# RWKV recurrence on one core: keys repeated by TensorE into PSUM, values repeated by DMA

## The chip, the cores and the metric

The kernel runs on one core of one Trainium2 chip. The metric is the device time of one execution in microseconds (us); the time before is the median of three runs. The core has five engines that work side by side and wait for each other by semaphores: TensorE (PE) multiplies matrices and writes to PSUM, VectorE (DVE) and ScalarE (ACT) work elementwise on SBUF and PSUM, GpSimd (POOL) elementwise on SBUF, and SyncE (SP) issues DMAs, as ACT does for stores.

## What is computed

Four layers run one after the other on x of 16 x 100 x 512 (fp32): a cross-attention (layer 0), an RWKV block (1), a second cross-attention with its feed-forward (2), and another RWKV block (3). The change touches the RWKV blocks alone. Their core, per batch, for 32 heads of 16 channels:

```python
def step(s, rkvw):
    r_t, k_t, v_t, w_t = rkvw
    a = k_t[..., :, None] * v_t[..., None, :]
    out = jnp.einsum('bhi,bhij->bhj', r_t, u * a + s)
    s = a + w_t[..., :, None] * s
    return (s, out)
...
_, out = jax.lax.scan(step, s0, rkvw)
```

Each head has a state of 16 x 16 (key channel i, value channel j) that decays by w and gains k times v in each of 100 time steps; r reads it out. Before it stand a layer norm, a mix with the previous step and projections to r, k, v, w and the gate g; after it a group norm, the gate, the output projection, and a channel mix (feed-forward).

## The kernel before

`rwkv` takes 16 batches in 4 groups of G = 4, so T = 400 columns (batch, time) in each tile. The 512 channels are 4 chunks of 128; chunk C of all 16 (group, chunk) pairs is 8 units, so there are 128 units a layer. A unit is two planes of 128 partitions x 400 columns: each partition is one (key channel, value channel) pair of a head, and one scan instruction of DVE runs its recurrence over the columns. Time step 0 of each batch has a decay of 0, so that four batches stand in one scan.

A unit has these steps, with the lines of the kernel before:

- `spread(u)` (L1132): two matmuls with 32 rows each write v, repeated by a selection matrix `sel` over the partitions, to the PSUM tile `vb` (two tiles of two banks each, in turn), shifted by one time step. ACT then copies the initial state s0 (`s0r`) to the first column of each batch.
- `product(u)` (L1147): DVE multiplies `vb` in place by `kr`, the keys repeated over the partitions.
- `scan(u)` (L1156): DVE runs two scans, with the decays `wr` and the products in `vb`, into the SBUF tile `a`; POOL multiplies `a` by `rr`, the repeated receptances.
- `gather(p)` (L1166): for each pair of units, four matmuls add the products up over the key channels to the PSUM bank `acc`. After a chunk, `norm` (L1178) reads it.
- `bonus` (L1110) adds the term with u.

The repeated `kr`, `wr` and `rr` come from DRAM: the projections are stored there (`store`, L806, issued by ACT) and loaded by SP in `enter` (L1089, plain tiles `kc`, `vc`, `rc`) and `repeat` (L1099: three tensors, four DMAs each, for half a chunk of four units). `gates` (L1203) loads g.

The units share the engines with all the rest of the block. A loop over u (L1231) writes the order of every engine out by hand: instructions on PE, DVE, ACT and POOL stay in program order (`keep_in_program_order`), while SP's DMAs may be put in order by the framework. In each turn the loop emits the steps of the units, then takes "pieces" from a list (projections of the next group, output projection, channel mix) until a budget `due` in us is used up. Three PSUM banks (`slots`) serve the pieces; a bank that DVE reads is read one turn later (`slots.begin`). The tails of a turn's pieces are therefore read by DVE ahead of the next unit's scans.

```python
due = min(due, 0.0) + (2.5 if 0 <= u < 29 else 2.95 if u < UNITS - 32 else 3.9)
due -= 0.45 * (u % 2) + 0.7 * (at in (2, 7)) if unit else 0.0
```

Of the kernel before, what the change touches and what calls it, by code (L numbers as in the profile page):

```python
# [17 lines left out]
G = 4  # L18
# [17 lines left out]
def xattn_sequence(ctx: ExitStack, tc: tile.TileContext, d: dict, out: bass.AP):  # L36
# [42 lines left out]
    vector, scalar, gpsimd = InOrder(nc.vector), InOrder(nc.scalar), InOrder(nc.gpsimd)  # L79
# [556 lines left out]
    def rwkv(n, ws, next_weights, last):  # L636
# [6 lines left out]
        with ExitStack() as es:  # L643
# [6 lines left out]
            vbs = [psum.tile([128, 2, 512], F32, name=f"vb{i}") for i in range(2)]  # L650
            acc = psum.tile([128, 512], F32, name="acc")
            slots = Slots([psum.tile([128, 512], F32, name=f"mm{i}") for i in range(3)])
            vec = rwkv_vecs(one, n)
# [35 lines left out]
            fold = one.tile([128, 32], F32, name="fold")  # L689
            nc.vector.tensor_reduce(fold, ident.rearrange("p (r s) -> p s r", s=32), AX.X, ALU.add)  # L690
            sel = one.tile([128, 16, 32], F32, name="sel")
            for j in range(16):
                nc.vector.tensor_copy(
                    sel[:, j, :].rearrange("p (h i) -> p h i", i=16),
                    fold.rearrange("p (h j) -> p h j", j=16)[:, :, j : j + 1].to_broadcast([128, 2, 16]),
                )


            share = one.tile([128, 2], F32, name="share")
            nc.vector.tensor_reduce(share, heads8.rearrange("p (q h) -> p h q", h=2), AX.X, ALU.add)  # L700
# [3 lines left out]
            for jg in range(4):  # L704
                nc.vector.tensor_copy(
                    gat[:, jg, :].rearrange("p (h g q) -> p g q h", g=4, q=4)[:, jg],
                    heads8.rearrange("p (q h) -> p q h", h=2),
                )
                nc.vector.tensor_tensor(
                    gat[:, jg, :].rearrange("p (h j) -> p h j", j=16),  # L710
                    gat[:, jg, :].rearrange("p (h j) -> p h j", j=16),
                    share[:, :, None].to_broadcast([128, 2, 16]), ALU.add,
                )

            s0r = one.tile([128, 4, NC, 4, B], F32, name="s0r")
            for r in range(4):
                rs = slice(32 * r, 32 * r + 32)
                ps = slots.bank()
                for c in range(NC):
                    for jq in range(4):  # L720
                        mm(
                            out=ps[32 * jq : 32 * jq + 32, c * 64 : (c + 1) * 64], lhsT=ident[rs, rs],
                            rhs=s0[rs, c].rearrange("p b (g q) -> p q g b", q=4)[:, jq],
                            start=True, stop=True,
                        )
                scalar.copy(s0r[:, r].rearrange("p c g b -> p (c g b)"), ps[:, : NC * 64])

            steps = lambda t: t.rearrange("p (b t) -> p b t", t=L)
            stage = lambda name: two.tile([128, 512], F32, tag="stage", bufs=6, name=name)
# [6 lines left out]
            nws = {}  # L736

# [60 lines left out]

            def projections(g, base):
                nm = f"{n}_{g}"  # L800
                to = put[g] = {
                    t: dram.tile([NC, 4, 32, T], F32, tag=t, name=f"d{t}_{nm}")
                    for t in ("k", "v", "r", "w", "g")
                }

                def store(t, c, tile):  # L806
                    nc.scalar.dma_start(out=to[t][c].rearrange("r p t -> (r p) t"), in_=tile)
# [83 lines left out]
                def plain(f, w, t, co):  # L891
                    def read(ps):
                        out = stage(f"{t}_{nm}_{co}")
                        scalar.copy(out[:, :T], ps[:, :T])
                        store(t, co, out[:, :T])

# [74 lines left out]
            def channels(g, slot):  # L971
# [41 lines left out]
                def keys(co):  # L1013
                    def read(ps):
                        if co == 0:
                            st["kk"] = two.tile([128, NC, T], F32, tag="kk", bufs=1, name=f"kk_{nm}")
# [19 lines left out]
                def values(i):  # L1036
                    b = g * G + i

                    def read(ps):
                        def add():  # L1040
# [3 lines left out]
                            if last:  # L1044
                                nc.sync.dma_start(out=out[b], in_=xb[b])
# [41 lines left out]
            products = {}  # L1087

            def enter(C):  # L1089
# [4 lines left out]
                for k, bufs in (("v", 2), ("k", 1), ("r", 1)):  # L1094
                    t[k] = two.tile([128, T], F32, tag=f"{k}c", bufs=bufs, name=f"{k}c_{n}_{C}")
                    nc.sync.dma_start(out=t[k], in_=put[g][k][c].rearrange("r p t -> (r p) t"))
                repeat(C, 0)

            def repeat(C, rp):  # L1099
                g, c = C // NC, C % NC  # L1100
                rep = chunks[C]["rep"][rp] = {}
                for t in ("k", "w", "r"):
                    rep[t] = two.tile([128, 2, T], F32, tag=f"{t}rep", bufs=3, name=f"{t}r_{n}_{C}_{rp}")
                    for jq in range(4):
                        nc.sync.dma_start(
                            out=rep[t][32 * jq : 32 * jq + 32],
                            in_=put[g][t][c, 2 * rp : 2 * rp + 2].rearrange("r p t -> p r t"),
                        )

            def bonus(C, part):  # L1110

                t, c = chunks[C], C % NC
                if part == 0:
                    t["rk"] = two.tile([128, T], F32, tag="rk", bufs=1, name=f"rk_{n}_{C}")
                    scalar.mul(t["k"], t["k"], vec["u"][:, c : c + 1])
                    gpsimd.tensor_tensor(t["rk"], t["r"], t["k"], ALU.mult)
# [12 lines left out]
            def where(u):  # L1129
                return u // 8, u % 8 // 2, u % 2  # L1130

            def spread(u):  # L1132

                C, jg, rp = where(u)
                p4 = vbs[u % 2][:, :, :T].rearrange("p r (b t) -> p r b t", t=L)
                for i in range(2):
                    rs = slice(64 * rp + 32 * i, 64 * rp + 32 * i + 32)
                    mm(
                        out=p4[:, i, :, 1:L], lhsT=sel[rs, 4 * jg : 4 * jg + 4, :].rearrange("p q m -> p (q m)"),
                        rhs=steps(chunks[C]["v"][rs, :])[:, :, 0 : L - 1], start=True, stop=True,  # L1140
                    )
                g = C // NC
# [579 lines left out]
```

## Time and profile before

| what | value |
|---|---|
| median of 3 runs | 3533.54 us (3524.69 to 3534.94) |
| profiled execution: time, span | 3530.07 us, 3528.3 us |
| mean granted TensorE clock | 0.935 |
| units of layer 1, of layer 3 | 867 to 1506 us, 2793 to 3431 us |
| DMA over the span | 216.60 MB, 61 GB/s |

The largest groups of instructions that belong to the recurrence:

```profile
L77 POOL TENSOR_TENSOR a<-a,rr 128x800 f32<-128x800 f32 x256 | 480.9, 1879 | 342.4 <-DVE a L77 269.7
L77 DVE TENSOR_TENSOR_SCAN a<-wr,vb 128x400 f32<-128x400 f32 x512 | 475.7, 971 | 19.8 <-PE acc L82 10.9
L77 DVE TENSOR_TENSOR vb<-vb,kr 128x792 f32<-128x792 f32 x256 | 250.5, 979 | 197.0 <-ACT vb L77 195.5
...
L82 PE MATMUL vb<-vc,sel 32*128 32x396 f32 x1024 | 261.0, 568 | 3.4 <-DVE a L77 2.2
...
L77 ACT COPY vb<-s0r 128x8 f32<-128x8 f32 x256 | 43.0, 168 | 408.7 <-PE vb L82 322.9
```

A row gives the line of the code (L77 and L82 are helpers through which most instructions pass), the engine, the operation, the tile written and those read, the shapes and the count; then the busy time of the group in us, the mean of one in ns, and the time that the engine stood idle just before them, with what ended it. Each fp32 matmul stands as two records, so 1024 records are 512 matmuls.

### The profile page before, as it was taken

How to read it: one execution, taken by the hardware profiler on the slowest of the kernel's cores; microseconds unless marked ns; L12 is line 12 of the kernel's file. 1: busy time of each engine (PE TensorE's matmuls, PEld its weight loads, DVE VectorE, ACT ScalarE, POOL GpSimd, SP SyncE). 2: the span in 40 equal slices, each digit the busy share in tenths (PEclk: the TensorE clock that was granted, in tenths of full speed). 3: DMA queues.
4: the chain of work that ended last, by engine and by line, in shares of the span. 5: the costliest groups of instructions: out<-in, count | busy, mean ns of one | idle time of the engine just before them, and what ended most of it. 6: DMA issues, size and time to landing. Idle time of an engine off the chain costs nothing. (4 is left out here: it accounts for less than half of the span.)

```text
span 3528.3 us, 46276 instructions
## 1 busy us (share of the span) xinstructions
PE 3217.1 (91%) x17795; PEld 1432.9 (41%) x17795; DVE 1770.8 (50%) x3570; ACT 981.8 (28%) x1715; POOL 1376.4 (39%) x1036
## 2 busy tenths in 40 slices
PE   6899998868999988988999999789998899998898
PEld 3444443333333333334454555345553333333333
DVE  4777777723777665514333333310001477775651
ACT  1322223222233233321322223211112233333232
POOL 1444444443666665511212111210002466665551
PEclk8999999978999989999999999999997899998998
DMA  5000001012434441101000010110012243433310
GB/s 169 21 31 21 31 21 33 1 56 86 126 108 124 126 146 54 38 27 55 25 19 19 19 31 18 39 53 8 10 57 68 87 129 104 134 115 117 87 29 14
DMA packets 153426, 216.60 MB, mean 61 GB/s; under 512 B 23498, under 2 KB 132106, under 8 KB 153206
## 3 DMA queue, kind: packets, MB, share of 16 engines
q1 hardware_dynamic: 130166, 180.87, 17.3%
q10 hardware_dynamic: 23040, 32.78, 2.6%
q8 instruction: 140, 2.29, 0.3%
q14 instruction: 80, 0.66, 0.1%
HBM read 174.25 MB, written 36.04 MB: 60 GB/s over the span
## 5 line engine op out<-in xcount | busy, mean ns | idle before, releaser
L77 POOL TENSOR_TENSOR a<-a,rr 128x800 f32<-128x800 f32 x256 | 480.9, 1879 | 342.4 <-DVE a L77 269.7
L77 DVE TENSOR_TENSOR_SCAN a<-wr,vb 128x400 f32<-128x400 f32 x512 | 475.7, 971 | 19.8 <-PE acc L82 10.9
L77 DVE TENSOR_TENSOR vb<-vb,kr 128x792 f32<-128x792 f32 x256 | 250.5, 979 | 197.0 <-ACT vb L77 195.5
L77 DVE CUSTOM_DVE_ANT_0 junk<-l_sc,mask 100x361 f32<-100x361 f32 x512 | 273.0, 533 | 90.1 <-PE l_sc L82 73.6
L82 PE MATMUL vb<-vc,sel 32*128 32x396 f32 x1024 | 261.0, 568 | 3.4 <-DVE a L77 2.2
L77 DVE TENSOR_TENSOR pt<-l_sc,maskT 121x400 f32<-121x400 f32 x384 | 193.5, 566 | 89.9 <-PE l_sc L82 89.0
L77 ACT ACTIVATE pt<-pt 121x1600 f32<-121x1600 f32 x96 | 147.6, 1538 | 282.2 <-DVE pt L77 280.7
L1425 DVE CUSTOM_DVE_ANT_0 junk<-l2a_sc,mask 100x361 f32<-100x361 f32 x256 | 136.9, 535 | 172.9 <-PE l2a_sc L82 155.7
L77 POOL TENSOR_TENSOR xj<-tm,ext 128x400 f32<-128x400 f32 x160 | 152.8, 962 | 174.3 <-DVE tm L77 168.0
L77 DVE SCALAR_TENSOR_TENSOR tm<-mm,vec,sx 128x400 f32<-128x400 f32 x160 | 99.9, 631 | 235.6 <-PE mm L82 190.9
L1461 POOL TENSOR_TENSOR pa<-pt,pt 121x1600 f32<-121x1600 f32 x16 | 57.2, 3574 | 366.8 <-ACT pt L1456 366.8
L63 PE MATMUL h<-yTb,l_fc 128*128 128x400 f32 x512 | 175.3, 505 | 8.2 <-ACT yTb L229 8.2
L1642 DVE TENSOR_TENSOR x<-pb,x 100x512 f32<-100x512 f32 x16 | 12.8, 799 | 338.3 <-DMA pb<-po 332.7
L82 PE MATMUL v<-l_v_w,ct 128*121 128x512 f32 x384 | 180.0, 613 | 0.0
L82 PE MATMUL k<-ct,l_k_w 128*128 128x361 f32 x512 | 173.0, 481 | 7.3 <-DVE mv_l2a L207 7.3
L77 POOL TENSOR_TENSOR pa<-pt,pt 121x1600 f32<-121x1600 f32 x32 | 114.7, 3586 | 165.5 <-ACT pt L77 165.5
L63 PE MATMUL p<-l_proj,h 128*128 128x512 f32 x384 | 165.4, 592 | 0.0
L77 ACT COPY vb<-s0r 128x8 f32<-128x8 f32 x256 | 43.0, 168 | 408.7 <-PE vb L82 322.9
L82 PE MATMUL l_sc<-kz,qz 32*100 32x361 f32 x1024 | 117.1, 528 | 42.6 <-DVE pt L77 21.7
L82 PEld LDWEIGHTS vb<-vc,sel 32*128 32x128 f32 x1024 | 84.8, 190 | 146.9 <-issue 107.3
L82 PE MATMUL mm<-l_Wo,gc 128*100 128x512 f32 x256 | 124.6, 629 | 8.4 <-POOL gc L77 8.4
L63 PEld LDWEIGHTS h<-yTb,l_fc 128*128 128x128 f32 x512 | 98.1, 192 | 83.3 <-ACT yTb L229 10.1
(258 smaller groups left out, 5305.6 us busy)
## 6 DMA issues: line engine op xcount, KB each, us to landing
kr<-dk SPq DMA_DIRECT2D x256, 100.0 KB
wr<-dw SPq DMA_DIRECT2D x256, 100.0 KB
rr<-dr SPq DMA_DIRECT2D x256, 100.0 KB
ct<-in_ctxT SPq DMA_DIRECT2D x32, 722.0 KB
dk<-k ACTq DMA_DIRECT2D x32, 200.0 KB
kc<-dk SPq DMA_DIRECT2D x32, 200.0 KB
dw<-wd ACTq DMA_DIRECT2D x32, 200.0 KB
dv<-v ACTq DMA_DIRECT2D x32, 200.0 KB
```

Source lines behind the costliest of these rows:

```text
L63: nc.tensor.matmul(out=ps, lhsT=lhs(c), rhs=rhs(c), start=(c == 0), stop=(c == n - 1))
L77: return lambda *args, **kw: tc.keep_in_program_order(op(*args, **kw))
L82: pin(nc.tensor.matmul(**kw))
L1425: nc.vector.tensor_tensor_reduce(out=junk, in0=ss[r][:L, :S2], in1=t["mask"], scale=-1.0, scalar=FLT_MAX, op0=ALU.add, op1=ALU.min, accum_ ...
L1461: nc.gpsimd.tensor_tensor(t["pa"], t["pt"][0], pt, ALU.add)
L1642: nc.vector.tensor_tensor(x, pb[:, i, :], x, ALU.add)
```

## The change

It alters who repeats what. The order of the units in a chunk becomes: first the four that share planes 0 and 1, then the four that share planes 2 and 3.

- Values: `fetch(u)` loads v for one unit from DRAM, repeated by two DMAs (200 KB each) into an SBUF tile `vr` (three buffers), two units ahead. The shift by one time step is made by storing v in DRAM one element further on. ACT's copy of s0 to the first columns (`first`) goes to this tile, one unit ahead.
- Keys: `keys_of(C, r)` repeats one plane of the keys by one 32-row matmul into a PSUM bank, one of three (`kbs`), for the four units that share it. The first column of the banks holds 1.0, set once.
- `recurrence(u)`: for each of the two planes, a product of 128 x 400 (vr in SBUF, keys in PSUM) into a PSUM bank `pr`, of which there is one, and then its scan.
- `wr` and `rr` are loaded by one DMA each with runs of 3200 bytes; `kr` is gone. The DRAM layout of k, v, r and w changes with it, so that each store and each plain load becomes four DMAs of 32 rows.
- SP's DMAs in the loop stay in program order now. The channel mix's weights come by quarters, as their buffers come free. `kk` moves to the ring `xm`; the tile `a` has eight buffers.
- The budgets of the loop are set anew.

The diff, cut to its core:

```diff
-    vector, scalar, gpsimd = InOrder(nc.vector), InOrder(nc.scalar), InOrder(nc.gpsimd)
+    vector, scalar, gpsimd, sync = map(InOrder, (nc.vector, nc.scalar, nc.gpsimd, nc.sync))
...
-            vbs = [psum.tile([128, 2, 512], F32, name=f"vb{i}") for i in range(2)]
+            kbs = [psum.tile([128, 512], F32, name=f"kb{i}") for i in range(3)]
+            pr = psum.tile([128, 512], F32, name="pr")
...
+            for kb in kbs:
+                vector.memset(steps(kb[:, :T])[:, :, 0], 1.0)
...
+            def rows_of(g, t, c):
+                if t == "g":
+                    return [(slice(0, 128), put[g][t][c].rearrange("r p t -> (r p) t"))]
+                rows = put[g][t][1:] if t == "v" else put[g][t]
+                rows = rows[c * 128 * T : (c + 1) * 128 * T].rearrange("(p r t) -> r p t", r=4, t=T)
+                return [(slice(32 * r, 32 * r + 32), rows[r]) for r in range(4)]
...
                 def store(t, c, tile):
-                    nc.scalar.dma_start(out=to[t][c].rearrange("r p t -> (r p) t"), in_=tile)
+                    for ps, rows in rows_of(g, t, c):
+                        nc.scalar.dma_start(out=rows, in_=tile[ps])
...
-            def repeat(C, rp):
+            def repeat(C, rp, names):
...
-                for t in ("k", "w", "r"):
-                    rep[t] = two.tile([128, 2, T], F32, tag=f"{t}rep", bufs=3, name=f"{t}r_{n}_{C}_{rp}")
-                    for jq in range(4):
-                        nc.sync.dma_start(
-                            out=rep[t][32 * jq : 32 * jq + 32],
-                            in_=put[g][t][c, 2 * rp : 2 * rp + 2].rearrange("r p t -> p r t"),
-                        )
+                for t in names:
+                    rep[t] = two.tile([128, 2, T], F32, tag=f"{t}rep", bufs=2, name=f"{t}r_{n}_{C}_{rp}")
...
+                    sync.dma_start(
+                        out=rep[t], in_=bass.AP(x.tensor, n0, [[4 * T, 32], [0, 4], [1, 2 * T]])
+                    )
...
             def where(u):
-                return u // 8, u % 8 // 2, u % 2
+                return u // 8, u % 4, u % 8 // 4
...
+            def fetch(u):
...
+                a = values[u] = two.tile([128, 2, T], F32, tag="vr", bufs=3, name=f"vr_{n}_{u}")
+                v = put[g]["v"]
+                for h in range(2):
+                    n0 = v.offset + (c * 128 + 64 * h + 16 * jg + 2 * rp) * T
+                    sync.dma_start(
+                        out=a[64 * h : 64 * h + 64],
+                        in_=bass.AP(v.tensor, n0, [[0, 16], [4 * T, 4], [1, 2 * T]]),
+                    )
...
+            def keys_of(C, r):
+                rs = slice(32 * r, 32 * r + 32)
+                mm(
+                    out=steps(kbs[(4 * C + r) % 3][:, :T])[:, :, 1:L], lhsT=rep4[rs, :],
+                    rhs=steps(chunks[C]["k"][rs, :])[:, :, 0 : L - 1], start=True, stop=True,
+                )
...
+            def recurrence(u):
                 C, jg, rp = where(u)
                 rep = chunks[C]["rep"][rp]
-                a = products[u] = two.tile([128, 2, T], F32, tag="a", bufs=4, name=f"a_{n}_{u}")
+                a = products[u] = two.tile([128, 2, T], F32, tag="a", bufs=8, name=f"a_{n}_{u}")
                 for i in range(2):
-                    vector.tensor_tensor_scan(
-                        a[:, i, :], rep["w"][:, i, :], vbs[u % 2][:, i, :T], 0.0, ALU.mult, ALU.add
-                    )
+                    kb = kbs[(4 * C + 2 * rp + i) % 3]
+                    vector.tensor_tensor(pr[:, :T], values[u][:, i, :], kb[:, :T], ALU.mult)
+                    vector.tensor_tensor_scan(a[:, i, :], rep["w"][:, i, :], pr[:, :T], 0.0, ALU.mult, ALU.add)
                 gpsimd.tensor_tensor(a, a, rep["r"], ALU.mult)
...
+                if 0 <= u + 2 < UNITS:
+                    fetch(u + 2)
                 if 0 <= u + 1 < UNITS:
-                    spread(u + 1)
-                if unit:
-                    product(u)
+                    first(u + 1)
                 slots.begin()
                 if unit:
-                    scan(u)
+                    recurrence(u)
+                C, at = u // 8, u % 8
+                if unit and at == 3:
+                    keys_of(C, 3)
+                elif at == 7 and 0 <= C + 1 < NC * NG:
+                    keys_of(C + 1, 1)
                 C, at = u // 8 + 1, u % 8
                 if 0 <= C < NC * NG:
                     if at == 4:
                         enter(C)
+                    elif at == 5:
+                        repeat(C, 0, "w")
                     elif at == 6:
-                        repeat(C, 1)
+                        repeat(C, 0, "r")
                         bonus(C, 0)
+                        keys_of(C, 0)
...
+                if unit and at == 0:
+                    keys_of(C, 2)
+                elif unit and at in (1, 2):
+                    repeat(C, 1, " wr"[at])
...
-                if u % 2 and 0 <= (u - 3) // 2 < UNITS // 2:
-                    gather((u - 3) // 2)
-
-                due = min(due, 0.0) + (2.5 if 0 <= u < 29 else 2.95 if u < UNITS - 32 else 3.9)
-                due -= 0.45 * (u % 2) + 0.7 * (at in (2, 7)) if unit else 0.0
+                if 0 <= u - 2 < UNITS and (u - 2) % 8 >= 4:
+                    gather(u - 2)
+
+                due = min(due, 0.0) + (2.93 if 0 <= u < 29 else 3.38 if u < UNITS - 32 else 4.3)
+                due -= 0.8 * (at in (6, 7, 0, 1)) + 0.7 * (at in (2, 7)) + 0.4 * (at in (0, 3, 6, 7)) if unit else 0.0
```

## The prediction

> **What bounds the kernel now.** I read the busy table and the slices of the page first, then the stage table over the recurrence of both RWKV layers, then the PE part of the timeline inside one unit, then who waits for the tile `vb`.
>
> ```profile
> PE 3217.1 (91%) x17795; PEld 1432.9 (41%) x17795; DVE 1770.8 (50%) x3570; ACT 981.8 (28%) x1715; POOL 1376.4 (39%) x1036
> ...
> PEclk8999999978999989999999999999997899998998
> ```
> ```profile
> 867.00:1002.00 135.00, 130.36 (x496) 49.43 (x493) 106.68 (x133) 43.21 (x93) 92.28 (x75) 0.92 0.38 114
> 1002.00:1151.00 149.00, 143.44 (x552) 54.23 (x552) 109.05 (x136) 49.48 (x103) 99.40 (x82) 0.95 0.39 115
> 1151.00:1316.00 165.00, 149.72 (x560) 56.86 (x556) 109.41 (x136) 53.38 (x109) 109.24 (x91) 0.90 0.44 131
> 1316.00:1506.00 190.00, 177.76 (x608) 65.11 (x605) 113.03 (x136) 64.68 (x127) 95.56 (x77) 0.93 0.18 50
> ```
> Columns: window, its length, busy us of PE, PEld, DVE, ACT, POOL (instructions), granted clock, DMA share, GB/s. The four rows are the four groups of 32 units of layer 1; layer 3 repeats them to within 1 us (2793 to 3431). A unit takes 135/32 = 4.2, 4.7, 5.2 and 5.9 us. PE is busy 97, 96, 91 and 94% of that, DVE 79, 73, 66 and 59%, POOL 68, 67, 66 and 50%. So PE sets the pace, and DVE is the next one, close behind in the first group: 3.33 us of 4.2.
>
> What of PE is the part that the change removes:
> ```profile
> 1105.43 0.96 DVE L77 TENSOR_TENSOR vb<-vb,kr 128x792 f32<-128x792 f32 x1
> ...
> 1106.53 1.86 DVE L77 TENSOR_TENSOR_SCAN a<-wr,vb 128x400 f32<-128x400 f32 x2
> ...
> 1106.70 0.94 PE L82 MATMUL vb<-vc,sel 32*128 32x396 f32 x4
> ...
> 1107.47 0.83 PE L82 MATMUL mm<-tz,td_maa_w 32*128 32x400 f32 x2
> ...
> 1108.23 2.95 PE L82 MATMUL mm<-xj,l_Wr 128*128 128x400 f32 x8
> ```
> Each matmul of fp32 stands as two records. The two matmuls of one spread (four records) lie in different row groups and start together: they hold PE 0.77 us here (1106.70 to 1107.47), 0.86 where the next is not a 32-row one. One 32-row matmul alone holds it 0.76 (1107.47 to 1108.23). So one repeat costs PE about what two side by side cost. Over both layers I counted 541 starts with `vb` in the trace, 0.43 us apart from the next at the median; in 84 of them a mix or gather runs along, so they cost nothing.
>
> On DVE, a scan that needs the product just made starts 1.10 us after the product's start (1105.43 to 1106.53), though the product took 0.96; two scans without such a tie take 1.86 together, 0.93 each. Without a tie, the next start comes before the end.
>
> ```profile
>   ACT vb L77: 355.3, 193
>   POOL a L77: 287.8, 170
>   DVE vb L77: 195.5, 107
> ```
> This is who waits for `vb`: ACT, then POOL and DVE. These waits are for an engine with spare time and pay nothing by themselves; they show that DVE stands behind PE in every unit.
>
> **What the Trainium skill says.** "SBUF — State Buffer", Who interferes with whom: a DVE instruction with at most one SBUF input does not contend with GpSimd. The trace agrees: scans take 954 to 989 ns whether POOL multiplies or not; the new form keeps one operand in PSUM, so neither engine should slow. "VectorE: DVE Perf Modes", The DRAIN you can't avoid: the next op does not start until the pipe is empty, and a read after write needs a semaphore; the trace shows the 0.14 us or so above. "TensorE: Matmul & The Clock Gate", Part 1: the clock halves after an idle window of about 3.4 us. The trace shows more than that:
> ```profile
> 900.00:914.00 14.00, 14.00 (x63) 4.37 (x62) 11.13 (x15) 7.37 (x14) 9.04 (x10) 1.00 0.41 123
> 914.00:928.00 14.00, 13.79 (x28) 4.55 (x26) 7.78 (x10) 4.11 (x9) 8.98 (x9) 0.51 0.24 75
> 928.00:942.00 14.00, 14.00 (x57) 5.71 (x56) 10.63 (x13) 3.28 (x10) 8.61 (x7) 1.00 0.57 169
> ```
> PE is busy 98% of the middle window and still runs at half clock, after a stretch of matmuls with 32 and 64 rows. Few rows count as little work, it seems; I use this only in the rivals.
>
> **The change, part by part.**
>
> (1) Spreads go. 541 - 84 = 457 starts x 0.43 us = 197 us less PE.
>
> (2) Keys come: four matmuls of 32 rows for 8 units, 128 in all over two layers, two starts each: 256 x 0.43 = 110 us. Some will run beside a 32-row mix, as 84 of the old did; I take 12 us off: 98. Net on PE: -99 us, 0.39 a unit.
>
> (3) DVE. One product of 792 becomes two of 400. The nearest row is `pt<-l_sc,maskT 121x400`, 566 ns, one operand in PSUM; now both scans hang on the product before, so each product costs 566 + 34 = 600 to the next start (34 ns is the gap between tied pairs in the timeline, a statistic and its aggregate for one). A scan with nothing tied behind it is 0.89 to the next start. So 2 x (0.60 + 0.89) = 2.98 a unit, against 0.92 (0.88 untied to 1.03 tied) + 2 x 0.89 = 2.70: +0.28. If the write to the single `pr` after the scan that reads it is also made to wait, two more ties of 0.12: +0.52 (upper end); +0.15 if the ties are hidden. I take 0.25. DVE per unit of the first group: 3.33 + 0.25 = 3.58, of the others 3.66 to 3.78.
>
> (4) Against that, PE per unit at the old clock is 4.2 - 0.39 = 3.8, 4.3, 4.8, 5.5 with its waits. In three of the four groups PE stays ahead of DVE by 0.6 us or more, and the whole 0.39 comes out. In the first, single chunks of 8 units stood at 3.76 and 3.95 us a unit (starts of the scans at 867.3, 897.3, 936.6, 968.3): there DVE's 3.55 to 3.7 is the limit and only about 0.2 comes. That takes 8 units x 2 chunks x 0.2 x 2 layers = 6 us off. Sum so far -93.
>
> (5) New waits of PE. `keys_of(C, 3)` and `keys_of(C + 1, 1)` write the bank that the first product of the very unit (at = 3, at = 7) reads. PE's whole queue stands behind it: the pieces of that iteration, and behind those ACT's reads and DVE's mixes. The product itself stands behind the reads of banks that PE filled in the iteration before. So where a mix came last, PE waits for a read (0.63 `tm`) and the product (0.60): 1.2 to 1.3 us. There are 2 x 32 = 64 such places; where chains of matmuls read by ACT came last, DVE is ahead and there is no wait. Before, the spread waited for a scan one unit back and was mostly late itself. Lower end 0, upper end all 64 at 1.3 = 83 us; I take about four in ten: +33 us. Without it the sum would be -93.
>
> (6) DMA. Per 8 units went out: keys, decays and receptances repeated, 6 x 400 KB; loads 800 and stores 1000 KB: 4.2 MB. Now 4 x 400 + 8 x 400 + 1800 = 6.6 MB, 825 KB a unit. The page gives q1 180.87 MB in 17.3% of 16 engines: 296 GB/s when busy. 845 kB at 296 is 2.9 us of 4.6: 62%, against 38 to 44 now. Hidden: three buffers `vr` let a transfer start when the unit three back has its product, some 1.3 units (6 us) before ACT's `first` needs it, and it takes 0.8 us of issue, about 1 to its first packet, and 1.4 of transfer. SP issues 33 in place of 28 per 8 units at 0.42, some 14 us of 37. On SP, now in written order, a fetch stands behind the twelve loads of `enter` and the load of `gates`; 13 x 0.38 = 5 us, which the 6 just cover. If the cover is gone, ACT stands in `first`, and behind it the evacuations that free PE's banks.
>
> (7) ACT issues 17 stores per 8 units in place of 5: 12 x 0.33 = 4 us on an engine that is 32% busy. Hidden, save beside the decays (two exponentials and four stores each, 2.4 us): 0 to 16 us, I take +3. Setup (the copies that built `sel`, 16 at 85 ns start to start, go; others come), `kk` in another ring, the weights by parts and the first-column copy (0.17 us on ACT, as now): nothing. ACT no longer waits for PE there, nor PE for it.
>
> Sum: -197 + 98 + 6 + 33 + 3 = -57; a little of PE's present waits on DVE (`vb` 2 to 8 us a layer) goes with the spreads: -63. The profiled execution has a span of 3528.3 and a time of 3530.1; so 3467. The median of the runs is 3.4 higher: 3470.
>
> **Rivals.**
>
> A, chance 0.53: the above, 3445 to 3505.
>
> B, the new waits hardly show and the denser mix holds the clock up: without (5), -96, and some of the half-clock windows go: 3425. For it: DVE stands idle 20% or more. Chance 0.12.
>
> C, DVE becomes the bound in more than two chunks, with the tie on `pr` (+0.52) and reads in bursts: 3.9 to 4.0 a unit in two groups. The gain shrinks to about 25: 3508. Against: groups 3 and 4 have 1.4 us and more of room. Chance 0.12, a third of it within 0.3% of before.
>
> D, slower: the waits of (5). Place: the two key matmuls per chunk; price: what DVE is behind there. The net of PE and DVE is -93, over 64 places 1.45 us each: from there on it turns. With a queue of two or three reads ahead of the product the wait is 1.9 to 2.5, and a window that drops to half clock costs 1.7 of its 3.4: at 2.3 us a place, 147 + 0 to 68 - 93 = about +70: 3600. For it: the dips after gaps of about 1 us in the trace. Against: most iterations end in a chain that ACT reads. Chance 0.17.
>
> E, transfers late: a fetch behind `enter`, `gates` or stores is later than 6 us. From a landing some 9 us after the buffer is free, three buffers pace the units themselves; +100: 3630. Chance 0.06. That the change doesn't do what it says I see no room for: the repeats are plain in the code.
>
> **How the numbers follow.** From about 0.3% (10 us) on, a measurement of this kernel can tell a change. Faster 0.53 + 0.12 + 0.08 = 0.73; within 0.3% 0.04; slower 0.17 + 0.06 = 0.23. The range 3410 to 3575 leaves out most of D and E and little below; the likeliest case's own is 3445 to 3505.
>
> **What would show it.** (1), (2): no `vb` on PE; a group of 256 records of keys, and in the stage table units of about 3.9, 4.4, 4.9 and 5.6 us. (3): products of about 566 ns, scans still near 970, DVE near 3.6 us a unit. (5): PE's waits at the key matmuls, DVE named, 30 us or so in all. (6): DMA share near 0.6 and hardly any wait of ACT for `vr`. Wrong: units paced by DVE at over 4 us, PE's clock well under 0.9, or `vr` among the waits.

## The result, and the profile after

The changed kernel takes 3616.93 us (median of four runs, 3614.93 to 3619.98) against 3530.0 for the kernel before on the same chip: ratio 1.0247, 95% interval 1.0228 to 1.0267. It is slower by 87 us, where 3470 was forecast. The profiled execution has a span of 3616.0 us (before 3528.3) and a mean granted clock of 0.911 (0.935).

The busy table, the slices and the first DMA queue of the page after:

```profile
PE 3235.0 (89%) x17027; PEld 1469.6 (41%) x17027; DVE 1853.9 (51%) x3812; ACT 976.2 (27%) x1715; POOL 1375.9 (38%) x1038
...
PEclk7999999968888988899999999899996889888998
...
q1 hardware_dynamic: 133030, 259.53, 24.1%
```

PE has 768 matmul records fewer and is busy 18 us *longer*. The row of the clock says why: from the ninth slice to the seventeenth and from the thirty-first to the thirty-seventh, where the units of layers 1 and 3 run, most digits are one lower than before.

The stage table of the four groups of layer 1 after (columns as in the prediction):

```profile
892.70:1044.00 151.30, 128.71 (x391) 49.27 (x393) 116.53 (x165) 42.41 (x92) 90.73 (x73) 0.83 0.61 178
1044.00:1201.00 157.00, 143.71 (x460) 54.65 (x456) 119.85 (x170) 49.28 (x104) 99.50 (x82) 0.88 0.58 173
1201.00:1376.50 175.50, 153.20 (x468) 57.70 (x464) 119.72 (x170) 54.43 (x113) 109.78 (x92) 0.83 0.61 179
1376.50:1558.60 182.10, 167.45 (x526) 61.96 (x518) 124.36 (x170) 62.73 (x125) 95.84 (x76) 0.91 0.39 113
```

The groups took 135, 149, 165 and 190 us before, at a clock of 0.95, 0.95, 0.90 and 0.93. Only the last is faster now. A unit takes 4.7, 4.9, 5.5 and 5.7 us, where 3.9, 4.4, 4.9 and 5.6 were foreseen; PE is busy 85, 92, 87 and 92%.

To add the difference up, I split PE's time in each stage in three: the time in which its records show it idle; the loss to half clock, which is half of the time in which PE is busy while the trace's clock record grants half speed; and the work, which is the rest, that is, what the busy time would have been at full clock.

| us | before | after | difference |
|---|---|---|---|
| units of layers 1 and 3, work | 562.0, 562.1 | 514.4, 516.0 | -93.8 |
| units, PE idle | 37.7, 37.5 | 72.8, 74.3 | +71.9 |
| units, PE busy at half clock | 77.9, 78.0 | 157.4, 138.1 | +139.6, a loss of 69.8 |
| matmuls of s0 in the setup | 2.9, 2.9 | 25.2, 25.2 | +44.7 |
| all the rest of the span | | | -4.9 |
| sum | | | +87.7 |

With the idle time in it, the units stand at half clock for 95.6 and 95.6 us before, 180.9 and 160.4 after. So PE was relieved of nearly the work that the prediction named (-94 of -99), and three things took it back and more: idle time of PE, half clock, and a setup that had been costed at nothing. The setup shows in a window over these matmuls, first of the kernel before, then after:

```profile
749.80:752.60 2.80, 2.80 (x128) 2.56 (x128) 0.00 (x0) 1.12 (x3) 0.40 (x2) 0.50 0.03 6
```
```profile
755.20:780.40 25.20, 25.18 (x128) 24.99 (x128) 0.00 (x0) 1.12 (x3) 0.47 (x3) 0.50 0.00 1
```

Both have 128 records of 64 columns at half clock. Before, a matmul was 32 x 32 and wrote one strip of 32 partitions, so that many ran side by side: a record took 290 ns in the mean, but there was one every 22 ns. Now each is 32 x 128 (`fold`), writes all 128 partitions, and four add up one after the other with the same 32 rows (a row group): 197 ns a record. It happens once a layer, and PE, ACT's reads of it and the first unit stand behind it.

The groups of the recurrence after:

```profile
L77 DVE TENSOR_TENSOR_SCAN a<-wr,pr 128x400 f32<-128x400 f32 x512 | 504.8, 986 | 19.4
L77 DVE TENSOR_TENSOR pr<-vr,kb 128x400 f32<-128x400 f32 x512 | 294.8, 576 | 72.5 <-ACT vr L77 54.3
...
L82 PE MATMUL kb<-kc,rep 32*128 32x396 f32 x256 | 140.5, 633 | 45.9 <-DVE pr L77 45.0
...
L77 ACT COPY vr<-s0r 128x8 f32<-128x8 f32 x256 | 49.2, 201 | 341.7 <-DMA vr<-dv 158.1
```

Of PE's 72.8 us of idle time in layer 1's units, 24.4 stand before the key matmuls (16 places, the longest 3.6 us), with DVE's product named; the kernel before had next to nothing there (2.2 for `vb`). ACT waits 158 us for the values; whether that matters is a question for an experiment.

### The profile page after: what moved, and what is told of

It is laid out like the page before. It is cut to its first block, busy times and chain, and to the rows that moved or that the text cites. A ratio compares the mean times of both kernels' runs of the same rounds, so it can differ in the third digit from the quotient of the medians.

```text
span 3616.0 us, 45914 instructions
## 1 busy us (share of the span) xinstructions
PE 3235.0 (89%) x17027; PEld 1469.6 (41%) x17027; DVE 1853.9 (51%) x3812; ACT 976.2 (27%) x1715; POOL 1375.9 (38%) x1038
## 5 line engine op out<-in xcount | busy, mean ns | idle before, releaser
L77 DVE TENSOR_TENSOR_SCAN a<-wr,pr 128x400 f32<-128x400 f32 x512 | 504.8, 986 | 19.4
L77 DVE TENSOR_TENSOR pr<-vr,kb 128x400 f32<-128x400 f32 x512 | 294.8, 576 | 72.5 <-ACT vr L77 54.3
L82 PE MATMUL kb<-kc,rep 32*128 32x396 f32 x256 | 140.5, 633 | 45.9 <-DVE pr L77 45.0
L82 PE MATMUL mm<-z,maa_w2a 32*128 32x400 f32 x256 | 127.6, 609 | 20.1 <-DVE tm L77 10.1
L82 PE MATMUL acc<-a,gat 128*32 128x400 f32 x1024 | 139.7, 591 | 3.8 <-POOL a L77 3.8
L77 ACT COPY vr<-s0r 128x8 f32<-128x8 f32 x256 | 49.2, 201 | 341.7 <-DMA vr<-dv 158.1
```

The source lines that it names most:

```text
L77: return lambda *args, **kw: tc.keep_in_program_order(op(*args, **kw))
L82: pin(nc.tensor.matmul(**kw))
```

## The experiments

Theory 1 holds that the loss has three separate sources: the setup matmuls; stretches of matmuls with few rows, which run at half clock now that the spreads no longer fill the other row groups; and DVE's pace, which PE's shorter turns now meet. The rivals: all of the half clock follows from the new idle time; the transfers of the values pace the units; or the key matmuls stand in the wrong place, and moving them ends the wait. Ratios are to the kernel before, run on the same chip.

**The setup side by side (e1).** The changed kernel with the setup matmuls in another order: the four row groups in turn, each into a bank of its own.

```diff
-            for r in range(4):
-                rs = slice(32 * r, 32 * r + 32)
-                ps = slots.bank()
-                for c in range(NC):
-                    for q in range(4):
+            s0banks = [*kbs, pr]
+            for c in range(NC):
+                for q in range(4):
+                    for r in range(4):
+                        rs = slice(32 * r, 32 * r + 32)
                         mm(
-                            out=ps[:, c * 64 : (c + 1) * 64], lhsT=fold[rs, q, :],
+                            out=s0banks[r][:, c * 64 : (c + 1) * 64], lhsT=fold[rs, q, :],
```

> Edit: only the permutation of the initial state before the first unit (mm<-s,fold, 128 records, 25.2 us in layer 1 against 2.8 of mm<-s,ident before) is done in four row groups side by side. Theory setup: about 22 us a layer of the 87 lost are these matmuls, so some 40 us come back, to about 3575. Rival (the whole loss is in the units, and the start of the units is set by something else): within 8 us of the changed kernel, 3609 to 3625.

3599.54 us (3596.43 to 3602.22), ratio 1.0196 (1.0177 to 1.0216): 17 us off. The matmuls fell from 25.2 to 7.1 us a layer, as the Trainium skill's "TensorEngine Tiling (Array Packing)", Key Properties, leads one to expect (row tiles work independently; its Gotcha 1 asks for a bank for each). The trace agrees: three records into the `kbs` and one into `pr` start within 0.05 us, and the next four 0.21 us later. But the stretch behind them, up to the first unit, grew by 6 to 7 us a layer. The window over the matmuls in this run, and the line of DVE that shows why:

```profile
751.30:758.50 7.20, 7.10 (x128) 6.94 (x128) 0.00 (x0) 0.00 (x0) 0.00 (x0) 0.50 0.01 2
```
```profile
759.01 0.06 DVE L77 MEMSET kb<- 128x4 f32 x1 [12.82 <-ACT s0r L77]
```

The banks used here are those of the keys. DVE's memsets of their first columns now wait for ACT's copies out of them, and the statistics of the layer norm stand behind the memsets; PE then waits 7.3 us for the normalised x, where it waited 1.3. So 36 of the 45 us of the setup's matmuls went, a wait of the edit's own took back some 12, and 17 came back in all; where the other 7 went, this run doesn't show.

**The keys later in the turn (e2).** The key matmuls of turns 3 and 7 are emitted at the end of the turn instead of right behind the recurrence.

```diff
-                C, at = u // 8, u % 8
-                if unit and at == 3:
-                    keys_of(C, 3)
-                elif at == 7 and 0 <= C + 1 < NC * NG:
-                    keys_of(C + 1, 1)
...
                     due -= take(p)
+                C, at = u // 8, u % 8
+                if unit and at == 3:
+                    keys_of(C, 3)
+                elif at == 7 and 0 <= C + 1 < NC * NG:
+                    keys_of(C + 1, 1)
                 u += 1
```

> Edit: the key matmuls of turns 3 and 7, which wait for DVE's product of the same unit, are issued at the end of the turn, behind its pieces. Theory waits: PE's 24 us a layer at kb go, and some windows at half clock with them: 3540 to 3580. Theory clock (few rows in the array, no matter the wait): half-clock time stays near 640 us and less than 20 us come back. Theory DVE (DVE sets the pace, PE only waits for it somewhere else): within 8 us of 3617.

3617.04 us, ratio 1.0245 (1.0219 to 1.0272): no change at all. PE's wait at the keys went, and stood elsewhere. From the waits of this run (engine and line waiting, what it waited for, us in all, times, longest):

```profile
PEld mm L82 <- POOL rk L77: 98.3, 26, 6.4
DVE pr L77 <- PE kb L82: 94.4, 36, 6.5
PE mm L82 <- POOL rk L77: 80.0, 26, 5.5
```

Now DVE waits for the keys, and PE for POOL's `rk` of the bonus; PE's wait for it had been 13.4 us. PE's work even fell by 12 to 14 us a layer, as more of the keys' time lay beside other matmuls (36 us of it alone on PE, 55 in the changed kernel), and its idle time rose by 18 to 22. So moving the keys to the end of the turn exchanges one wait for another; a place in between was not tried.

**The keys over 128 rows (e3).** The key matmul contracts all 128 rows; its weights are zero in the rows of the other planes. Work, count and order stay.

```diff
-            rep4 = one.tile([128, 128], F32, name="rep4")
+            rep4 = one.tile([128, 4, 128], F32, name="rep4")
+            nc.gpsimd.memset(rep4, 0.0)
...
-                    out=steps(kbs[(4 * C + r) % 3][:, :T])[:, :, 1:L], lhsT=rep4[rs, :],
-                    rhs=steps(chunks[C]["k"][rs, :])[:, :, 0 : L - 1], start=True, stop=True,
+                    out=steps(kbs[(4 * C + r) % 3][:, :T])[:, :, 1:L], lhsT=rep4[:, r, :],
+                    rhs=steps(chunks[C]["k"])[:, :, 0 : L - 1], start=True, stop=True,
```

> Edit: the key matmuls contract over all 128 rows, with zeros in the rows of the other three planes; same columns, same result. Theory clock (the clock follows how many rows work): the half-clock time of 646 us falls by 60 us or more and the kernel gains 20 to 60 us. Rival (only idle time of PE halves the clock): half-clock time within 30 us of 646, time within 8 us of 3617; it can even lose, since a 128-row matmul can't run beside a 32-row one.

3587.38 us (3573.19 to 3592.62), ratio 1.0156 (1.0126 to 1.0186): 30 us off, from zeros alone. In the profiled execution, the fastest of the four, the time at half clock fell from 646 to 503 us over the whole trace, in layer 1's units from 180.9 to 105.8. One chunk, the second of the second group (8 units), shows it; the window of it before, after, and in this run:

```profile
1039.40:1080.90 41.50, 40.91 (x136) 12.98 (x137) 28.02 (x35) 12.17 (x25) 22.44 (x20) 0.92 0.41 122
```
```profile
1087.50:1130.40 42.90, 41.09 (x112) 13.03 (x111) 30.69 (x42) 12.04 (x26) 22.55 (x21) 0.82 0.56 167
```
```profile
1071.70:1112.30 40.60, 37.04 (x125) 12.64 (x124) 30.74 (x42) 12.03 (x26) 22.95 (x21) 1.00 0.61 175
```

The changed kernel keeps PE busy 96% of the chunk and gets a clock of 0.82; with the zeros it is busy 91%, with more idle time, and gets the full clock. So idle time alone doesn't decide it. The timeline of PE (start, us, what, records) in the same stretch, before and after:

```profile
1068.67 0.60 PE L82 MATMUL mm<-z,maa_w2a 32*128 32x400 f32 x1
1068.69 0.59 PE L82 MATMUL vb<-vc,sel 32*128 32x396 f32 x1
1069.11 0.49 PE L82 MATMUL mm<-z,maa_w2a 32*128 32x400 f32 x1
1069.12 1.15 PE L82 MATMUL vb<-vc,sel 32*128 32x396 f32 x3
```
```profile
1112.19 0.94 PE L82 MATMUL mm<-tz,td_maa_w 64*128 64x400 f32 x2 [0.59 <-ACT tz L77]
1113.06 0.93 PE L82 MATMUL mm<-z,maa_w2a 32*128 32x400 f32 x2
1113.92 0.94 PE L82 MATMUL mm<-tz,td_maa_w 64*128 64x400 f32 x2
1114.79 1.03 PE L82 MATMUL mm<-z,maa_w2a 32*128 32x400 f32 x1
1114.80 1.02 PE L82 MATMUL kb<-kc,rep 32*128 32x396 f32 x1
```

Before, spreads worked in other rows beside and between the mixes. After, mixes of 32 and decays of 64 rows stand alone from 1112.2 to 1114.8; there the clock is halved, just as a key matmul comes to run beside a mix, and it stays so for 17.07 us; in the kernel before, the dip in this stretch lasted 6.83.

But this chunk is not the common case. The trace's clock record changes in steps of 3.41 us only, so I looked at the 3.41 us before each fall to half clock in the units of both layers and asked whether PE was idle for more than a fifth of them.

| falls to half clock in the units: how many, us at half clock | before | after | e3 |
|---|---|---|---|
| behind idle time | 14, 140 | 31, 277 | 31, 181 |
| with PE busy for four fifths or more | 6, 51 | 4, 65 | 4, 41 |

Nearly all of the new half clock begins behind idle time. In the changed kernel, 19 of the 20 steps at full clock in which PE was idle for more than half were followed by a fall; of the 201 in which it was busy for over 97%, none. What the zeros changed is how long a fall lasts: the 31 behind idle time take 8.9 us each in the mean after, 5.8 in e3. One place in both runs, the window before the fall and the stretch at half clock, after and in e3:

```profile
1217.20:1220.62 3.42, 1.30 (x3) 0.59 (x4) 3.37 (x6) 0.20 (x1) 1.87 (x2) 1.00 0.62 173
1220.62:1227.45 6.83, 6.78 (x11) 2.82 (x10) 6.46 (x9) 3.70 (x4) 6.64 (x7) 0.50 0.33 101
```
```profile
1196.18:1199.59 3.41, 1.28 (x4) 0.59 (x4) 3.36 (x6) 0.20 (x1) 1.86 (x2) 1.00 0.51 145
1199.59:1203.00 3.41, 3.40 (x6) 1.49 (x5) 3.31 (x5) 2.36 (x3) 3.41 (x5) 0.50 0.02 4
```

In both, PE has waited 2.1 us for DVE, and a mix and a key matmul run at this place. The clock falls in both, and with the key over 128 rows it is back after one step instead of two. The Trainium skill's "TensorE: Matmul & The Clock Gate", Part 1, says that the gate goes by how busy PE has been recently. The falls behind idle time agree; the six and four falls with PE busy, and the longer falls with few rows, show that the time in use is not the whole of it. So the rival that half clock follows from the new idle time is right about where most falls begin, and wrong about how long they last.

**All three (e4).** e1, e2 and e3 together.

> The three edits together. If they act on different parts, their gains add to within 20 us: by theory setup 40, waits 40, clock 40 about 3500, faster than before; if clock and waits are one cause seen twice, about 3540.

3591.57 us, ratio 1.018 (1.0156 to 1.0203): no better than e3 alone. With the late keys in, PE has 97 and 102 us of idle time in the two layers' units (87 in each in e3), and the trace 563 us at half clock (503 in e3).

**The queue of SP (e5, e6).** e5 is the changed kernel with the twelve plain loads of a chunk spread over turns 4 (k), 5 (r) and 6 (v), so that the values of the unit at turn 7 are no longer issued behind all of them; e6 joins e1, e3 and e5.

```diff
                     elif at == 5:
+                        plain_load(C, "r", 1)
                         repeat(C, 0, "w")
                     elif at == 6:
+                        plain_load(C, "v", 1)
                         repeat(C, 0, "r")
```

> Edit: the twelve plain loads of the next chunk, issued together in turn 4, are spread: four of k in turn 4, four of r in turn 5, four of v in turn 6. Theory queue (SP in written order holds the values of unit 7 behind the loads, 4.4 us late at the mean, and with them DVE's product and PE's key matmul of turn 7): fetch 7 is late by under 1 us, PE's wait at kb falls from 24 us a layer to under 12, ACT's wait for vr clearly, time 3570 to 3600. Theory distance (PE and DVE are simply out of step at turns 3 and 7): kb stays near 24 us and the time within 10 us of 3617.

> Setup in four row groups, key matmuls of 128 rows and spread loads together. If the three causes are separate, their gains add: 17 + 30 + that of the loads (20 to 45): 3525 to 3550, about as fast as before. If idle time of PE only moves, 3565 or more.

e5: 3610.92 us, but with runs from 3596.37 to 3621.27; ratio 1.0247 (1.0223 to 1.0272). The issue of that fetch came 1.3 us after its buffer was free instead of 4.7 (means), but that of the second unit of a chunk 3.3 us instead of 1.9, so that part of the lateness only moved. Little followed: 6 us, which these runs can't tell from none. e6: 3543.52 us (3539.75 to 3547.24), ratio 1.0047 (1.0032 to 1.0062). That is 73 us off in all, more than the 53 of the three alone; why they add up to more, no run separates. Against the kernel before, the units of e6 have 97 us less work of PE, 89 more of idle time (78.6 and 85.2 us in the two layers) and 17 more of loss to half clock (116.1 us at half clock in each layer).

**Mixes over 64 rows (e7).** e6 with the mixes contracted over 64 rows, half of them zeros, and one buffer less for `a`.

```diff
-                    rs = slice(32 * f, 32 * f + 32) if f < 4 else slice(64, 96)
+                    if f < 4:
+                        rs, w, z = slice(64 * (f // 2), 64 * (f // 2) + 64), w2a[:, f % 2], st["z0"]
```

> As the run before, and the mixes for k, w, v and r contract over 64 rows, half of them zeros, in place of 32 (one buffer of the tile a less, to make room). Theory clock: half-clock time of a layer's units falls by another 20 us or more, time 10 to 30 us under the run before. Rival (rows don't matter, e3 was faster for another reason): no change; the mixes can no longer run beside a neighbour in the same row groups, so it may lose up to 10 us.

3545.03 us, ratio 1.005 (1.0035 to 1.0065), 499 us at half clock: nothing in sum. But the falls with PE busy, five with 48 us in e6, are gone, and those behind idle time rose from 26 with 184 us to 31 with 242. So 64 rows may be enough for the first kind; whether the missing buffer brought the second (see e14), this run doesn't separate.

**Mixes over 128 rows in the kernel before (e8, e15).** e8 has nothing of the change. The mixes contract 128 rows with zeros; to make room `kk` moves to the ring `xm`, which e15 does alone.

```diff
-            w2a = one.tile([128, E], F32, name="maa_w2a")
-            nc.sync.dma_start(out=w2a, in_=d[f"L{n}_maa_w2"][0:128, :])
+            w2a = one.tile([128, 4, E], F32, name="maa_w2a")
+            nc.gpsimd.memset(w2a, 0.0)
+            for f in range(4):
+                fs = slice(32 * f, 32 * f + 32)
+                nc.sync.dma_start(out=w2a[fs, f, :], in_=d[f"L{n}_maa_w2"][fs, :])
...
+                        mm(out=ps[:, :T], lhsT=w2a[:, f, cols], rhs=st["z0"], start=True, stop=True)
```

> The kernel BEFORE, with its mixes for k, w, v and r contracting over 128 rows, three quarters of them zeros (kk in the ring xm, to make room). Theory clock: the half-clock time of 95.6 us in each layer's units falls by a third or more, though the mixes lose their neighbours (84 starts shared with spreads, up to 36 us of PE): time 3500 to 3535. Rival (clock follows idle time only): half-clock time the same, time 3540 to 3565.

> The kernel before with one buffer moved (kk into another ring) and nothing else: the control for e8_before_mixes128, which made room for its weights in this way. Theory 1: no difference from before, within 5 us (3525 to 3535), so that the 25 us of e8 belong to the rows of its mixes. Rival: the ring itself gave it: 3505 to 3515.

e8: **3503.17 us** (3500.5 to 3507.14), ratio 0.9933 (0.9918 to 0.9948); e15: 3528.89, ratio 0.9994 (0.9985 to 1.0003). So the 25 us belong to the rows. The time at half clock fell from 459 to 376 us, and the group of the mixes in this run says the rest:

```profile
L82 PE MATMUL mm<-z,maa_w2a 128*128 128x400 f32 x256 | 109.9, 527 | 2.7 <-ACT z L77 2.4 <-ACT ew L77 0.3
```

The same 256 records were 582 ns each with 32 rows in the kernel before, and no longer run beside a spread: 64 of them had started within 0.1 us of another matmul, now none does. PE's work in the units rose by 9 us a layer for that. They still win by the clock: the six falls with PE busy (51 us) are gone, and behind idle time there are 12 with 137 us, for 14 with 140. This version beats both kernels.

**One product or fewer loads left out (e9, e10, e11).** On e6: e9 leaves out the second product of each unit, so that both scans read the first one's. e10 leaves out three of four loads of values and the first-column copies with them. e11 leaves out both.

```diff
-                    vector.tensor_tensor(pr[:, :T], values[u][:, i, :], kb[:, :T], ALU.mult)
+                    if i == 0:
+                        vector.tensor_tensor(pr[:, :T], values[u][:, i, :], kb[:, :T], ALU.mult)
```

> Base: the run with setup, 128-row keys and spread loads (3543). Left out: the second of the two products of every unit (the second scan takes the first one's product again), so the output is not the reference's; DVE has 0.6 us less in each unit. Theory DVE (what PE still idles, 80 us a layer against 38 before, is DVE's pace at the turns that are short on PE): PE's idle time in the units falls to under 50 us a layer, kb waits to under 8, time 3470 to 3510. Theory transfers (DVE is held by late values): idle stays above 65, time 3520 or more.

```diff
             def fetch(u):
...
+                if u % 4:
+                    values[u] = values[u - 1]
+                    return
```

> Same base. Left out: three of four loads of the values and of their first-column copies; four units take the same values, so the output is not the reference's; DMA traffic falls by 77 MB. Theory transfers: PE's idle time falls to under 50 us a layer, time 3470 to 3510. Theory DVE: idle stays above 65, time 3525 to 3545.

> Both left out at once. If DVE's pace and the transfers each cost something, below both runs before by what the other gains; if one of them is all of it, equal to that one within 8 us.

e9: 3494.5 us, ratio 0.9902 (0.9886 to 0.9918), 49 us less than e6. e10: 3536.61, 1.0024 (1.0016 to 1.0032), 7 less. e11: 3483.04, 0.9869 (0.9852 to 0.9885). The product left out makes DVE busy 172 us less, on an engine that is busy half of the span, and that brings 49, of which 40 are idle time of PE in the units; the transfers bring next to nothing, though ACT had waited 158 us for them. The key matmuls of e9 beside those above:

```profile
L82 PE MATMUL kb<-kc,rep 128*128 128x396 f32 x256 | 128.7, 589 | 22.5 <-DVE pr L77 22.5
```

PE's wait for DVE there halves, and its idle time in layer 1's units falls from 78.6 to 62.1 us. Not to 37.7, as before the change, though DVE is now busy 2.95 us a unit in the first chunk, less than the 3.28 before: some 21 to 24 us a layer of idle time beyond that remain in e11 (59.0) and e9, and come from neither the second product nor the transfers. That part stays open; the order of the pieces and their new budgets were not varied.

**Values earlier (e12).** e6 with `fetch` three units ahead and `first` two, four buffers `vr`, seven of `a`.

```diff
-                if 0 <= u + 2 < UNITS:
-                    fetch(u + 2)
-                if 0 <= u + 1 < UNITS:
-                    first(u + 1)
+                if 0 <= u + 3 < UNITS:
+                    fetch(u + 3)
+                if 0 <= u + 2 < UNITS:
+                    first(u + 2)
```

> Same base, full computation: values fetched three units ahead and their first columns written two units ahead, four buffers (seven of the tile a). Theory transfers: gains 20 us or more, under 3525. Theory DVE: within 8 us of 3543.

3548.42 us, ratio 1.0057 (1.0041 to 1.0073): nothing gained, as e10 has it.

**The clock held up in both (e13, e14).** e13 is e6 with the mixes of e8, and fewer buffers for `a`, `stage` and `tm` to make room; e14 has the fewer buffers alone.

```diff
-tag="a", bufs=8
+tag="a", bufs=7
...
-tag="stage", bufs=6
+tag="stage", bufs=5
...
-tag="tm", bufs=4
+tag="tm", bufs=3
```

> The changed kernel with the setup matmuls of s0 side by side, keys and mixes both contracted over 128 rows with zeros, the loads spread, and fewer buffers for a, stage and tm to make room. What it asks: does the change pay once the granted clock is held up in both kernels alike (to be set against e8_before_mixes128, 3503 us)? Theory 1 (clock and pace): the mixes give here what they gave before the change, 24 us at most, since half of the windows they cure are cured by the keys already: 3520 to 3535, half clock about 430 us, and the idle time of PE in the units stays at 75 us or more per layer, because DVE's pace sets it: the change still loses to e8. Rival (the clock was all that kept it back): below 3500, idle time as before or less.

> e13_all_held_up without the mixes over 128 rows: the control for its fewer buffers of a, stage and tm. Theory 1: the buffers cost nothing, the time is that of e6_setup_keys128_loads within 6 us (3538 to 3550). Rival: fewer buffers tie PE's pieces to later reads, 10 us or more slower than e6 (over 3553).

e14: 3564.8 us, ratio 1.0102 (1.0072 to 1.0133); e13: 3548.16, ratio 1.0046 (1.0032 to 1.0061). The fewer buffers cost some 20 us against e6, which I hadn't expected, and the mixes give 17 back. Compared with e8 (0.9933), the change still loses 1.1% with the same zeros in both; with the 20 us of the buffers put back it would stand, by my estimate, at about 3528, 25 behind e8. But the zeros don't give both the same clock. In both, no fall with PE busy is left; behind idle time e13 has 32 with 208 us, e8 12 with 137. In e13's units PE has 510 us of work a layer, 61 less than in e8, and 94 us of idle time against 36: of the 61 us a layer that the change saves on PE, 58 go in waits, and the half clock behind them costs another 36 us over both layers. Whether the change would lose at an equal clock, these runs don't show.

## Why the prediction was wrong

From the -63 us of the sum to the +87 measured it is 150 us. Half clock is 70 of them, the setup 45, idle time beyond what steps (4), (5) and (7) gave 36, work less relieved than foreseen 5, and all the rest takes 5 off.

- **Step that failed: the clock.** The sum took PE's time at the old clock, though the prediction itself had shown a window 98% busy at half clock, and said that few rows seem to count as little work. It used that only in the rivals. Measured: 70 us lost in the units. As the traces have it, the new waits begin most of that (31 falls behind idle time for 14), and few rows make the falls long: e3 has as many falls, and they are shorter. Steps (1) and (2) put 128 matmuls of 32 rows in the place of 512, and the fill between the mixes went; of the falls with PE busy, which that would explain, there are no more than before (4 for 6, 65 us for 51). That zeros in the idle rows bring the clock back is shown by e3 and e8; the part of the missing spreads stays open, as no run put them back. So the prediction priced the waits and left out what they do to the clock.
- **Step (7), "Setup ... nothing".** It went through the copies that build `sel`, not through the matmuls that use `fold`: the same 128 records a layer took 25.2 us for 2.9, 45 us in all. The diff showed it: 32 partitions of output had become 128, and a start by itself four that add up.
- **Steps (1) and (2) were right within 5 us**: -94 us of PE's work for -99, -47.6 in one layer and -46.1 in the other.
- **Step (3), mis-sized.** From a product to its scan 0.613 us pass at the median (0.60 taken), but from a scan to the next product 1.021, where 0.89 was taken: the write to the one `pr` does wait for the scan that reads it. A unit's products and scans thus take 2 x (0.613 + 1.021) = 3.27 us, against 1.07 + 0.90 + 0.88 = 2.85 before, where a tied product is followed by its scans: +0.42, near the upper end of 0.52 and not the 0.25 taken (+0.57 against the 2.70 that the step took for before). DVE's busy time, in which overlaps count once, rose by 0.33 a unit (437.9 to 480.5 us in layer 1); in the four groups it is 3.64, 3.75, 3.74 and 3.89 us a unit.
- **Steps (4) and (5), mis-sized and read too narrowly.** They gave 6 and 33 us to DVE's pace, 3 to ACT in (7), and took off 6 for waits on `vb`: 36 of new idle time. It was 72. The wait at the keys was close (45.0 in the page's row), but only part of it: moved away in e2, it came back at `rk`. That DVE's pace makes these waits e9 shows for about half of the new idle time (40 us of the 89 in e6); 43 to 49 us stay open. My reading, which no run tests, is that chunks at 4.4 us a unit leave DVE, at 3.6 to 3.8 busy, no room to make up in one turn what it loses in another: step (4) compared only averages.
- **Step (6) was right**: the DMA share is 0.58 to 0.61 in three groups, and the transfers are worth 7 us (e10). ACT's waits for `vr`, named as a sign against the forecast, were no such sign.
- **Rival D** had the sign and about the time (3600), with half clock in it, but not the mechanism: its 64 waits came to 45 us, not 147. It was the only rival to charge half clock to the waits, at 0 to 68 us; the 70 measured agree with that in size, but few rows, which e3 shows to count for most of it, are not in it. Rival C named the tie on `pr` and the bound by DVE, and gave it only about 40 us.

## What to carry to other kernels

Before matmuls are taken off TensorE, look at what they run beside and at the waits that come in their place: here PE's waits of a few us were followed by half clock, matmuls with few rows kept it there, and half clock took back 70 of the 94 us saved. Zeros up to 128 rows are a cheap remedy, worth trying in any kernel whose slices of the clock row fall below 9 while PE is busy. When the first engine is relieved, work out the second one's time from start to start, ties included, chunk by chunk, since its small waits become the first engine's. And price the setup: matmuls that used to write 32 partitions each side by side and now write all 128 can come one after the other.

## What the runs showed of the hardware

- The granted clock goes by PE's idle time and by its rows. In the changed kernel 31 of 35 falls came behind a window of 3.41 us with PE idle for more than a fifth of it, and none behind 201 with PE busy for over 97%; in the kernel before, 4 falls came behind 278 such busy windows. The same matmuls in the same order with 128 rows in place of 32, the added ones multiplying zeros, took the time at half clock from 646 to 503 us (keys, e3: as many falls, shorter ones) and from 459 to 376 (mixes, e8: no fall with PE busy left).
- A matmul with 32 rows can start together with others, one with 128 did not: of 256 records of the mixes, 64 started within 0.1 us of another matmul, none with 128 rows (e8); of the keys 20, and none (e3). So the zeros change two things at once, and these runs don't tell which of them moves the clock.
- A record of a matmul with 32 rows and 64 columns costs 197 ns at half clock when those of one row group follow each other, and 55 ns (7.1 us over 128) when four row groups take turns with a bank each.
- Two DVE instructions tied through one PSUM bank start 0.613 us apart for a product of 0.576 (read after write) and 1.021 for a scan of 0.986 (write after read): either tie costs about 36 ns, where two scans of 0.97 without one start 0.90 apart.
